# A four-layer graph network on one core: the first two quads of graphs in another order

## The chip, the cores and the metric

One core of a Trainium2 chip runs the whole program. Its engines work side by side, each through its own queue in program order: TensorE (PE; its weight loads are shown apart as PEld), VectorE (DVE), ScalarE (ACT), GpSimd (POOL) and SyncE (SP, which here only starts transfers). They wait for each other through semaphores. The metric is the device time of one execution in microseconds (us), the median of several runs; less is better. All data is 32-bit floating point.

## What is computed

128 graphs share one adjacency matrix of 128 nodes; each node has 256 features. Four layers follow each other, each with a residual and a normalization over the features:

```python
x = _layernorm(x + attention(x))     # layer 0: 512 edges, 4 heads; softmax over a node's edges; @ W_out.T
x = _layernorm(x + slconv(x))        # layer 1: three products with (adj*adj) @ . @ W1, W2, W3, relu between
x = _layernorm(x + split(x))         # layer 2: diagonal, upper, lower part of adj, each with its own W, + bias
x = _layernorm(x + gcn(x))           # layer 3: A_hat @ x, two products, batch norms over all graphs
```

In layer 0 an edge's score is `sum(a * leaky_relu(q[src] + q[dst])) + log(adj[src, dst] + 1e-8)`, the softmax runs over the edges that leave a node, and the weighted values are summed per node. Layer 3 normalizes over all graphs, so its end can only follow when all graphs are through its first part.

## The kernel before

The 128 graphs are taken in 32 groups of four, called quads. A pipeline works on several quads at once: `iteration(k)` does layer 1 of quad k, layers 2 and 3 of quad k - 1, the output of layer 0 of quad k + 1, the softmax of quad k + 2 and the query products of quad k + 3. Before that steady part stand `start()`, which loads everything, sorts the edges and takes the first quads through layer 0, and `iteration_0()`, which fills the pipeline. After it comes a last part for the batch norms and the output. The order of every engine's queue is the order in which the program writes the instructions (`manual_schedule`); no scheduler changes it. Tiles come from pools with a fixed number of buffers; a tile whose turn comes again waits until its last reader is done. [...]

The steps that the change and the prediction speak of, with the lines of the kernel before:

- `values_in(k)` (L235 on) transposes a quad on TensorE (L245) and copies it out (L247); `values(k, i)` makes queries and values of one graph (L259, copies at L260 and L261). After the last graph the queries are written to DRAM (L268), by SP or by POOL.
- `gather_one` (L336) fetches the queries of an edge's source rows, and then adds those of its target rows, by indirect transfers from POOL: chunk c of 128 edges needs a transfer for the sources (t = 0) and an adding one for the targets (t = 1). `gather` does chunks 0 to 2, `gather_last` chunk 3, which takes over a buffer of an earlier chunk.
- `score(k, c)` (L368, L370, L371) turns a gathered chunk into scores on VectorE: three passes over 128 x 1024 elements. L373 adds the edge weights of quads 0 and 1, L375 those of the later quads, after the last chunk.
- `sorted_scores` (L360) brings the scores of quads 0 and 1 into the sorted order with a permutation matrix that lies in the room of w3; so w3 can be loaded only when quad 1 is sorted. Later quads are gathered in sorted order already, and one transpose (L385, with copies at L387) does instead.
- `softmax_parts` (L389 to L400): two scans on VectorE for the maximum, a subtraction, an exponential on ScalarE (L396, which needs another table of functions), two scans for the sum. `attention` transposes the result (`pat`, L408) and divides (L410, L412).
- `scatter` (L418) writes the weights into a matrix in DRAM with four indirect transfers from POOL, each of which waits for the one before; `load_weights` (L427) reads it back through SP; `by_row` (L437) makes rows of it (ScalarE, or VectorE for quad 0); `aggregate` (`py`, L451) multiplies it with the values.
- `stage_a` (`po`, L465) is layer 0's output product, the residual (L468) and the norm (L106 to L121) for two graphs, then for the other two.
- `mix1` (`pm`, L476), `first` (`ph`, L490) and `mix2`/`mixed` (L532, L540 to L544) are layer 1's first product for quad 0; `first_seven` does the same for later quads with seven products instead of eight. `late_sums` (L548, L549), `second` (L575, seven products of blocks again; `between[i]` holds work that is put between its steps) and `third` (`p3`, L655), `third_mix` (L668), `third_norm` follow.
- `weight_blocks` (L188 to L191), `hidden_sums` and `second_sums` (L181 to L184) make the sums of weight blocks that the seven-product form needs, on VectorE.
- In `start()`: the first ten products on `warm` (L1091), `late_loads` with its small vectors for biases and batch norms (L1143, L1149), the copy at L1253 with which POOL waits for quad 0's weights.

Of the kernel before, what the change touches and what calls it, by code (L numbers as in the profile page):

```python
# [11 lines left out]
AF = mybir.ActivationFunctionType  # L12
# [14 lines left out]
def gnn_stack(ctx: ExitStack, tc: tile.TileContext, x, adj, w_qv_t, a, w_out_t, src, dst,  # L27
# [14 lines left out]
    nc = tc.nc  # L42
# [3 lines left out]
    P = 128  # L46
# [18 lines left out]
    def ps(name):  # L65
        return psum.tile([P, 512], F32, tag="ps", name=name)
# [57 lines left out]
    def layer_norm(pool, r):  # L124
        mv = norm_stats(pool, r)
        norm_apply(pool, r, mv, norm_root(pool, mv))


    with ExitStack() as phase:
# [210 lines left out]
        def gather_last(k):  # L340
            quads[k].z[NE - 1] = z_buffer(k, NE - 1)
            for t in range(2):
                gather_one(k, t, NE - 1)
# [113 lines left out]
        def stage_a(k):  # L457

            s = quads[k]
            yts = s.yts  # L460
            for j in range(0, QB, 2):
                po = ps("po").rearrange("p (b d) -> p b d", d=D)
                for t in range(2):
                    for dc in range(DC):
                        nc.tensor.matmul(po[:, t, :], yts[j // 2][:, t, dc, :], wo[:, dc, :],  # L465
                                         start=(dc == 0), stop=(dc == DC - 1))
                xj = s.xr[:, j:j + 2, :]
                nc.vector.tensor_add(xj, xj, po)  # L468
                layer_norm(wk, xj)
# [553 lines left out]
        def iteration_0():  # L1023

            late_sums(0)
            between = {i: [] for i in range(14)}
            between[0] = [lambda: attention(1), lambda: scatter(1)]
            for c, i in ((0, 1), (1, 3), (2, 6)):
                between[i].append(lambda c=c: score(2, c))
            between[1].append(lambda: gather_last(2))  # L1030
            for j, i in enumerate((10, 11, 12, 13)):
                between[i].append(lambda j=j: by_row(1, j))
            second(0, between)
            score(2, NE - 1)
            gather(3)
            rest = third(0, 0)
            next(rest)
            first_seven.blocks = weight_blocks(w1_sb, w1_s)
            layer2.blocks = weight_blocks(l2w, l2w_s)
            next(rest)  # L1040
            aggregate(1)
            queries.blocks = weight_blocks(wqv, wqv_s)
            hidden_sums()
            for _ in rest:
                pass
            stage_a(1)
            third_mix(0, 0)
            rest = third(0, 2)
            next(rest)
            third_norm(0, 0)  # L1050
            mix1(1, 0)
            mix1(1, 2)
            next(rest)
            w = first_seven(1)
            steps = softmax_parts(2)
            for _ in range(4):
                next(steps)
            w.p1()
            next(steps)
            run(w.p5, w.p2)  # L1060
            for _ in steps:
                pass
            next(rest)
            attention(2)
            scatter(2)
            score(3, 0)
            gather_last(3)
            w.p6()
            next(rest, None)
            w.p7()  # L1070
            third_mix(0, 2)
            w.p4()
            w.p3()
            quads[0].layer2 = layer2(0, 1)
            next(quads[0].layer2)
            third_norm(0, 2)
            next(quads[0].layer2)

        def start():
# [9 lines left out]
            warm = ps("warm")[:, :N]  # L1089
            for _ in range(10):  # L1090
                nc.tensor.matmul(warm, ones, ones, start=True, stop=True)  # L1091
# [47 lines left out]
            def late_loads():  # L1139
                for c in range(DC):  # L1140
                    nc.sync.dma_start(l2w[:, c, :].rearrange("p (k f) -> p k f", k=3),
                                      l2_w[:, c * P:(c + 1) * P, :].rearrange("k p f -> p k f"))
                nc.sync.dma_start(bias, bass.AP(tensor=l2_bias.tensor, offset=l2_bias.offset, ap=[[0, P], [1, D]]))  # L1143
                nc.sync.dma_start(w3_sb, w3.rearrange("(c p) f -> p c f", p=P))
                nc.sync.dma_start(l3w1, l3_w1_t.rearrange("(c p) f -> p c f", p=P))
                quads[4].xg = load_x(4, "xg", 1, xpool)
                for t, vecs in ((bn1, (l3_b1, l3_g1, l3_be1)), (bn2, (l3_b2, l3_g2, l3_be2))):
                    for i, ap in enumerate(vecs):
                        nc.sync.dma_start(t[:, i, :], ap.rearrange("(c p) -> p c", p=P))  # L1149

# [21 lines left out]
            nc.vector.scalar_tensor_tensor(weight, picked, LOG_EPS, count, op0=ALU.add, op1=ALU.mult)  # L1172
            nc.scalar.activation(weight, weight, AF.Ln)
# [11 lines left out]
            values_in(1, quads[1].xr, nc.scalar.copy)  # L1185
# [22 lines left out]
            score(0, NE - 1, ends[:, 3, :])  # L1208
            sorted_scores(0, perm, (NE - 1,))
# [16 lines left out]
            values_in(2, quads[2].xr, nc.scalar.copy)  # L1226
# [4 lines left out]
            nc.vector.tensor_add(an, a_sb, ident)  # L1231
            attention(0)
            values(2, 0, nc.scalar.copy, qt=l3w1_s.rearrange("p t f -> p (t f)").rearrange("p (b d) -> p b d", d=D))
# [10 lines left out]
            values(2, 1, nc.scalar.copy)  # L1244
            pr = ps("col_ps")[:, :1]
            nc.tensor.matmul(pr, an, ones[:, 0:1], start=True, stop=True)
            nc.vector.tensor_add(sums[:, 2:3], sums[:, 0:1], pr)
            nc.vector.tensor_sub(sums[:, 3:4], sums[:, 2:3], sums[:, 1:2])
            nc.scalar.activation(sums[:, 4:5], sums[:, 3:4], AF.Sqrt)
            score(1, 0, ends[:, 3, :])  # L1250
            values(2, 2, nc.scalar.copy)
# [3 lines left out]
            for c in (2, 3):  # L1255
                for t in range(2):
                    gather_one(1, t, c, cols_i[:, t, :])
            dinv = sums[:, 5:6]
            nc.vector.reciprocal(dinv, sums[:, 4:5])
            nc.vector.tensor_scalar(diag, an, dinv, None, op0=ALU.mult)  # L1260
            values_in(3, quads[3].xg, nc.scalar.copy)
            values(3, 0, nc.scalar.copy)
# [3 lines left out]
            score(1, 1, ends[:, 3, :])  # L1266
            values(3, 1, nc.scalar.copy)
            second_sums()
            for j in range(QB):
                by_row(0, j, None if j == 2 else nc.vector.tensor_copy)  # L1270
            aggregate(0)
            stage_a(0)
            values(3, 2, nc.scalar.copy)
            values(3, 3, nc.scalar.copy)
            mix1(0, 0)
            mix1(0, 2)
            score(1, 2, ends[:, 3, :])
            sorted_scores(1, perm, range(NE - 1))
            first(0, 0)
            score(1, NE - 1, ends[:, 3, :])  # L1280
            gather(2)
            first(0, 1)
            mixed(0, 0, mix2(0, 0))
            sorted_scores(1, perm, (NE - 1,))
            late_loads()
            first(0, 2)
            mixed(0, 1, mix2(0, 1))
# [3 lines left out]
            first(0, 3)  # L1291
            next(steps)
            mixed(0, 2, mix2(0, 2))
# [323 lines left out]
```

## Time and profile before

| | us |
|---|---|
| median of 3 runs (lowest, highest) | 3142.03 (3140.09, 3143.48) |
| the profiled execution's own time | 3137.62 |
| its span in the trace | 3135.9 |
| mean granted clock of TensorE | 0.995 of full speed |

The last three numbers belong to one execution, and rows of the profile are compared with its own time. What each engine did in stretches of the beginning (busy us, clock granted to TensorE, mean share of time in which the transfer engines were busy):

| stretch, us | TensorE | VectorE | ScalarE | POOL | clock | transfers |
|---|---|---|---|---|---|---|
| 30 to 40 | 8.93 | 9.79 | 3.16 | 0.78 | 1.00 | 0.13 |
| 40 to 50 | 4.21 | 8.18 | 1.57 | 5.34 | 0.77 | 0.74 |
| 50 to 60 | 9.65 | 5.05 | 4.94 | 3.79 | 0.89 | 0.19 |
| 60 to 70 | 2.70 | 8.85 | 2.38 | 3.49 | 0.79 | 0.42 |
| 70 to 80 | 9.41 | 3.92 | 1.47 | 2.59 | 0.70 | 0.62 |
| 80 to 90 | 8.86 | 9.33 | 2.55 | 4.60 | 1.00 | 0.70 |
| 90 to 100 | 10.00 | 5.25 | 3.67 | 4.65 | 1.00 | 1.01 |
| 100 to 110 | 6.61 | 8.85 | 2.31 | 1.75 | 1.00 | 1.03 |
| 120 to 130 | 10.00 | 3.20 | 5.51 | 3.54 | 1.00 | 0.84 |
| 140 to 150 | 7.57 | 8.67 | 2.12 | 1.43 | 1.00 | 0.64 |
| 150 to 160 | 4.02 | 8.30 | 3.71 | 1.33 | 0.90 | 0.00 |
| 160 to 170 | 9.99 | 7.19 | 2.91 | 4.01 | 0.76 | 0.01 |
| 190 to 200 | 10.00 | 9.47 | 2.69 | 0.00 | 1.00 | 0.00 |

In the rows of a timeline the first number is the start from the beginning of the span, the second the length; then come the engine, the line of the kernel, the operation, what it writes and reads with the shapes, the number of records (one matrix product of these types has two), and in brackets the idle time ahead of it with what ended it. A row of waits has the total in us, the number of waits and the longest one.

### The profile page before, as it was taken

What the parts mean: (1) busy time and instruction counts of PE and PEld (TensorE: products, weight loads), DVE (VectorE), ACT (ScalarE), POOL (GpSimd) and SP (SyncE); (2) the same over time, 40 slices, a digit from 0 to 9 for tenths busy, and PEclk for the clock granted to TensorE, in tenths of its full rate; (3) what the DMA queues carried; (4) which work ended last, traced back from release to release, by engine and by line L of the source; (5) the groups of instructions that cost most, each with busy time, mean ns of one, the idle gap of its engine ahead of it and who ended that gap; (6) DMA issues with size and microseconds to landing.
All of it is one profiled execution on the core that took longest, in us unless ns stands there. A gap on an engine that the chain in (4) does not pass through costs nothing. (4 is left out here: it accounts for less than half of the span.)

```text
span 3135.9 us, 39741 instructions
## 1 busy us (share of the span) xinstructions
PE 3070.0 (98%) x14752; PEld 2399.9 (77%) x14752; DVE 2307.2 (74%) x4600; ACT 1375.0 (44%) x2548; POOL 649.8 (21%) x535
## 2 busy tenths in 40 slices
PE   7899999999999999999999999999999999999987
PEld 3678888888888888888888888888888887874444
DVE  7777777777777777777777777777777776458888
ACT  3344433444444444443444444444343444326668
POOL 2311222222111111222222111111222220001135
PEclk8999999999999999999999999999999999999999
DMA  5623333333333323333333333223333331005557
GB/s 175 166 71 86 102 108 95 108 108 106 104 81 108 95 80 93 104 102 101 108 108 105 84 101 107 91 79 95 108 102 101 108 108 41 21 28 203 176 191 276
DMA packets 117473, 340.04 MB, mean 108 GB/s; under 512 B 14881, under 2 KB 51617, under 8 KB 108961
## 3 DMA queue, kind: packets, MB, share of 16 engines
q0 software_dynamic: 44544, 147.88, 19.4%
q1 hardware_dynamic: 70976, 188.71, 16.9%
q8 instruction: 117, 1.92, 0.3%
q10 hardware_dynamic: 1760, 0.92, 0.1%
q14 instruction: 76, 0.61, 0.1%
HBM read 252.00 MB, written 85.46 MB: 108 GB/s over the span
## 5 line engine op out<-in xcount | busy, mean ns | idle before, releaser
L575 PE MATMUL ph<-m,w 128*128 128x256 f32 x2048 | 473.4, 379 | 0.0
L655 PE MATMUL p<-w,h 128*128 128x256 f32 x2048 | 464.2, 380 | 0.0
L575 PEld LDWEIGHTS ph<-m,w 128*128 128x128 f32 x2048 | 386.7, 190 | 77.9 <-issue 14.8
L655 PEld LDWEIGHTS p<-w,h 128*128 128x128 f32 x2048 | 389.9, 190 | 67.0 <-issue 8.1
L336 POOL DMA_INDIRECT zs<-qd,src_idx x120 | 116.1, 968 | 1344.3 <-DMA qd<-qt 1214.1
L575 PE MATMUL ph<-m,w_s 128*128 128x256 f32 x1536 | 357.5, 379 | 0.0
L575 PEld LDWEIGHTS ph<-m,w_s 128*128 128x128 f32 x1536 | 291.8, 190 | 52.9 <-issue 14.8
L336 POOL DMA_INDIRECT zs<-qd,dst_idx x120 | 188.4, 1570 | 350.5 <-DMA zs<-qd,src_idx 325.3
L581 ACT COPY u<-ph 128x512 f32<-128x512 f32 x128 | 74.8, 584 | 354.9 <-PE ph L575 354.9
L418 POOL DMA_INDIRECT attd<-at,att_idx x128 | 140.7, 1099 | 353.1 <-DMA attd<-at,att_idx 251.5
L591 ACT ACTIVATE h<-h 128x512 f32<-128x512 f32 x192 | 121.2, 631 | 135.6 <-DVE h L587 135.6
L113 ACT ACTIVATE ln_sd<-ln_mv,eps 128x2 f32<-128x2 f32 x192 | 56.0, 291 | 280.2 <-DVE ln_mv L108 276.4
L370 DVE TENSOR_TENSOR zs<-zs,a_bc 128x1024 f32<-128x1024 f32 x125 | 153.1, 1225 | 4.3
L371 DVE TENSOR_REDUCE scores<-zs 128x16 f32<-128x1024 f32 x125 | 152.5, 1220 | 4.3
L718 ACT COPY x2k<-y 128x384 f32<-128x384 f32 x192 | 91.8, 478 | 138.6 <-PE y L711 114.3
L368 DVE SCALAR_TENSOR_TENSOR zs<-zs 128x1024 f32<-128x1024 f32 x125 | 151.4, 1212 | 1.1 <-DMA zs<-qd,dst_idx 1.1
L106 DVE BATCH_NORM_STATS2 ln_st<-xr 128x6 f32<-128x256 f32 x384 | 144.5, 418 | 6.6
L121 DVE TENSOR_SCALAR xr<-xr,ln_mv,ln_rs 128x256 f32<-128x256 f32 x384 | 143.3, 415 | 7.0
L587 DVE TENSOR_TENSOR h<-ph,u 128x512 f32<-128x512 f32 x128 | 87.1, 680 | 73.2 <-PE ph L575 54.9
L437 ACT COPY adc<-ad 128x512 f32<-128x512 f32 x125 | 133.4, 1067 | 5.5 <-DMA ad<-attd 5.5
L679 POOL TENSOR_TENSOR xb<-xr,bias 128x512 f32<-128x512 f32 x64 | 99.3, 1551 | 150.9 <-DVE xr L121 141.6
L532 PE MATMUL pm<-wt_t,h 128*128 128x128 f32 x1024 | 126.7, 277 | 0.0
(346 smaller groups left out, 6064.1 us busy)
## 6 DMA issues: line engine op xcount, KB each, us to landing
ad<-attd SPq DMA_DIRECT2D x32, 1024.0 KB, 4.8
zd<-z SPq DMA_DIRECT2D x31, 1024.0 KB, 7.5
zl<-zd SPq DMA_DIRECT2D x62, 512.0 KB, 3.8
xr<-in_x_dram SPq DMA_DIRECT2D x32, 512.0 KB, 7.3
x3d<-xr SPq DMA_DIRECT2D x32, 512.0 KB, 2.6
x3l<-x3d SPq DMA_DIRECT2D x32, 512.0 KB, 5.9
out_dram<-x3l POOLq DMA_DIRECT2D x31, 512.0 KB
qd<-qt SPq DMA_DIRECT2D x30, 512.0 KB, 2.6
```

Source lines behind the costliest of these rows:

```text
L106: nc.vector.bn_stats(st[:, i, :], r[:, i, :])
L121: nc.vector.tensor_scalar(r[:, i, :], r[:, i, :], mv[:, i, 0:1], rs[:, i:i + 1], op0=ALU.subtract, op1=ALU.mult)
L336: nc.gpsimd.indirect_dma_start(out=s.z[c], out_offset=None, in_=s.qd, in_offset=bass.IndirectOffsetOnAxis(ap=idx[:, c:c + 1], axis=0), com ...
L368: nc.vector.scalar_tensor_tensor(z, z, SLOPE, z, op0=ALU.mult, op1=ALU.max)
L370: nc.vector.tensor_mul(z3, z3, a_bc.unsqueeze(1).to_broadcast([P, QB, D]))
L371: nc.vector.reduce_sum(s.es[:, c, :], z.rearrange("p (r d) -> p r d", d=DH), axis=AX.X)
L418: nc.gpsimd.indirect_dma_start(out=ad, out_offset=bass.IndirectOffsetOnAxis(ap=att_idx[:, c:c + 1], axis=0), in_=s.at[:, c, :], in_offset= ...
L437: (copy or nc.scalar.copy)(s.adc[:, j * H:(j + 1) * H, :], s.ad.rearrange("p (s r) -> p r s", r=R)[:, j * H:(j + 1) * H, :])
L532: nc.tensor.matmul(pm[:, c // 2, c % 2, :], quads[k].h1[i, c], wt_t, start=True, stop=True)
L575: nc.tensor.matmul(bank[g][:, i].rearrange("p b n -> p (b n)"), wa[:, c, f:f + P], s.m2[:, blk_b, c].rearrange("p b n -> p (b n)"), start= ...
L591: nc.scalar.activation(h, h if src_ is None else src_, AF.Relu)
L655: nc.tensor.matmul(p3[:, t * D:(t + 1) * D], s.h2[f // 2][:, f % 2, j + t, :], w3_sb[:, f, :], start=(f == 0), stop=(f == K2 - 1))
```

## The change

Only `start()`, `iteration_0()` and `stage_a` are touched; the steady part and the end stay as they are. Nothing is computed otherwise. It does these things:

- `stage_a` falls into `out_product` (L462) and `out_norm` (L471), which for quad 0 are called apart: both products stand ahead of the first norm.
- In `start()`, quad 1's transposes go ahead of the logarithm, quad 2's transposes ahead of the last sorting product of quad 0, three of quad 2's four products ahead of quad 0's attention, and all of quad 3's products ahead of quad 0's weights; quad 3's queries are written to DRAM by POOL instead of SP.
- Two chunks of quad 1 are gathered in the order source, source, target, target instead of source, target, source, target.
- The scores of quad 1 go ahead of two small sums on VectorE that wait for a product of TensorE.
- Twenty products without use, of the kind of the first ten, stand ahead of quad 0's `aggregate`, and four ahead of its `mix1`.
- Quad 0's first layer-1 products are put in another order, and quad 1's four sorting products stand together behind them.
- The late loads follow behind these sorting products, w3 first; the small vectors go behind `second(0)` (`small_loads`). The weight sums of w1, l2w and l3w1 are put into `iteration_0` in other places, those of wqv into `start()`.
- In `iteration_0`, quad 1's attention and scatter stand behind three steps of `second(0)` instead of one; the scores of quad 2 are spread otherwise; `third(0, 0)` is issued in one piece; quad 2's softmax begins ahead of quad 1's output of layer 0.

```diff
-            between[0] = [lambda: attention(1), lambda: scatter(1)]
-            for c, i in ((0, 1), (1, 3), (2, 6)):
+            for c, i in ((0, 0), (1, 3), (2, 6)):
                 between[i].append(lambda c=c: score(2, c))
-            between[1].append(lambda: gather_last(2))
-            for j, i in enumerate((10, 11, 12, 13)):
-                between[i].append(lambda j=j: by_row(1, j))
+            between[2] += [lambda: attention(1), lambda: scatter(1)]
+            between[3].append(lambda: gather_last(2))
             second(0, between)
+            small_loads()
+            first_seven.blocks = weight_blocks(w1_sb, w1_s)
+            layer2.blocks = weight_blocks(l2w, l2w_s)
+            rest = third(0, 0)
+            next(rest)
             score(2, NE - 1)
             gather(3)
-            rest = third(0, 0)
-            next(rest)
-            first_seven.blocks = weight_blocks(w1_sb, w1_s)
-            layer2.blocks = weight_blocks(l2w, l2w_s)
-            next(rest)
-            aggregate(1)
-            queries.blocks = weight_blocks(wqv, wqv_s)
-            hidden_sums()
+            for j in range(QB):
+                by_row(1, j)
             for _ in rest:
                 pass
+            hidden_sums()
+            aggregate(1)
+            steps = softmax_parts(2)
+            for _ in range(4):
+                next(steps)
             stage_a(1)
             third_mix(0, 0)
             rest = third(0, 2)
             next(rest)
             third_norm(0, 0)
+            next(steps)
             mix1(1, 0)
+            next(rest)
             mix1(1, 2)
+            w = first_seven(1)
             next(rest)
-            w = first_seven(1)
-            steps = softmax_parts(2)
-            for _ in range(4):
-                next(steps)
             w.p1()
-            next(steps)
-            run(w.p5, w.p2)
             for _ in steps:
                 pass
-            next(rest)
+            run(w.p5, w.p2)
+            next(rest, None)
             attention(2)
             scatter(2)
+            w.p6()
             score(3, 0)
             gather_last(3)
-            w.p6()
-            next(rest, None)
...
+            score(1, 1, ends[:, 3, :])
...
             second_sums()
+            keep_running(20)
             for j in range(QB):
                 by_row(0, j, None if j == 2 else nc.vector.tensor_copy)
+            queries.blocks = weight_blocks(wqv, wqv_s)
             aggregate(0)
-            stage_a(0)
-            values(3, 2, nc.scalar.copy)
-            values(3, 3, nc.scalar.copy)
+            po = [out_product(0, j) for j in (0, 2)]
+            out_norm(0, 0, po[0])
+            keep_running(4)
             mix1(0, 0)
+            out_norm(0, 2, po[1])
+            first(0, 0)
+            score(1, 2, ends[:, 3, :])
+            first(0, 1)
             mix1(0, 2)
-            score(1, 2, ends[:, 3, :])
-            sorted_scores(1, perm, range(NE - 1))
-            first(0, 0)
+            mixed(0, 0, mix2(0, 0))
+            first(0, 2)
             score(1, NE - 1, ends[:, 3, :])
             gather(2)
-            first(0, 1)
-            mixed(0, 0, mix2(0, 0))
-            sorted_scores(1, perm, (NE - 1,))
+            first(0, 3)
+            mixed(0, 1, mix2(0, 1))
+            sorted_scores(1, perm)
             late_loads()
-            first(0, 2)
-            mixed(0, 1, mix2(0, 1))
+            pm = mix2(0, 2)
             steps = softmax_parts(1)
             for _ in range(4):
                 next(steps)
-            first(0, 3)
+            mixed(0, 2, pm)
             next(steps)
-            mixed(0, 2, mix2(0, 2))
             mixed(0, 3, mix2(0, 3))
             for _ in steps:
                 pass
```

`keep_running(n)` issues n products of `ones` with `ones` into a bank that nothing reads.

## Prediction

> **What bounds the kernel now.** I read the page first, then TensorE's own waits over the first 175 us, then the timeline of each engine there, then the stage windows.
>
> ```profile
> span 3135.9 us, 39741 instructions
> PE 3070.0 (98%) x14752; PEld 2399.9 (77%) x14752; DVE 2307.2 (74%) x4600; ACT 1375.0 (44%) x2548; POOL 649.8 (21%) x535
> ```
>
> TensorE is busy for 98% of the span, and after 174 us its timeline has no wait until the tail. Up to 174 us it has these (us in total, times, longest):
>
> ```profile
> PE pat L408 <- DVE pair L400: 14.8, 3, 6.0
> PE py L451 <- DVE adc L437: 7.9, 1, 7.9
> PE pe L360 <- DVE scores L373: 2.6, 2, 1.5
> PE pm L476 <- DVE xr L121: 2.4, 2, 1.8
> ```
>
> In TensorE's timeline (start, length, what, idle before it):
>
> ```profile
> 47.96 0.63 PE L408 MATMUL pat<-ident,pair 48*128 48x48 f32 x4 [5.37 <-DVE pair L400]
> 48.52 5.48 PE L259 MATMUL pq<-wqv,xt 128*128 128x512 f32 x8
> ...
> 70.59 3.68 PE L451 MATMUL py<-adc,m 128*64 128x128 f32 x32 [7.89 <-DVE adc L437]
> 74.20 4.61 PE L465 MATMUL po<-wo,yt 128*128 128x256 f32 x16
> ...
> 104.99 0.41 PE L408 MATMUL pat<-ident,pair 48*128 48x48 f32 x4 [3.39 <-DVE pair L400]
> ...
> 160.01 0.63 PE L408 MATMUL pat<-ident,pair 48*128 48x48 f32 x4 [5.99 <-DVE pair L400]
> ...
> 173.47 0.67 PE L697 MATMUL pt<-ident,xr 128*128 128x128 f32 x4 [1.22 <-DVE xr L121]
> ```
>
> The same products are slower after a long wait: eight pq take 5.48 here and 3.68 at 53.98; py takes 3.68 here and 1.97 at 131.43. The granted clock (third number from the end of a stage row; then the share of busy transfers, and GB/s) says why:
>
> ```profile
> 44.00:46.00 2.00, 0.00 (x0) 0.00 (x0) 1.58 (x6) 1.31 (x3) 1.46 (x2) 0.83 0.32 127
> 64.00:66.00 2.00, 0.00 (x0) 0.00 (x0) 1.97 (x3) 0.00 (x0) 0.00 (x0) 0.95 0.75 315
> 102.00:104.00 2.00, 0.00 (x0) 0.00 (x0) 1.97 (x4) 0.28 (x1) 0.00 (x0) 1.00 1.03 234
> ```
>
> So all there is to win is some 30 us of waits and half clock before 174 us. From there the work is the same and TensorE-bound, so the time moves one for one with the start of the last transposes that wait, now at 173.47. I walk the new order of each in-order queue to that instruction, with the durations and start-to-start distances of these rows.
>
> **1. Up to the first softmax (48 us): nothing.** Copying quad 1's transposes ahead of the logarithm frees TensorE 1.4 us earlier (24.99 to 23.57), but VectorE runs without a gap from 22.3 to 41.5 and the product at 40.42 waits for it. Quad 2's transposes (1.04) and three of its products (5.3) go into the 5.37 us ahead of pat. That wait shrinks to about 1 us, pat stays at 47.96, and the half clock of 45.3 to 52.1 goes. VectorE still makes quad 0's attention by 49.4.
>
> **2. Quad 0's weights (66.1 us): unmoved.** The four scatters (49.73, 54.11, 56.53, 59.14), the load at 61.26 and its arrival at 66.13, which ScalarE's copy shows, hang on that attention and on nothing moved. What moves is VectorE: score(1,0) waited at 54.42 for col_ps, a tiny product queued behind two pq. Now it needs only its gather, and the transfers are busy until 52 with both gathers, so the first has landed near 50.5. Scores 0 and 1 end at 58.6 (not 65.2), the four sums of w2 (4.67) at 64.3 (not 69.9), before the weights arrive. VectorE's first copy (0.62) lets py start at 66.75, not 70.59: 3.84 won.
>
> **3. Clock and quad 0's norms.** Twenty warming products (40 records; pm's show 0.12 each when fast) run from 59.3 to about 63.9 and leave 2.9 us idle. Cost if the cover were gone: at half clock they take 8 us (the first ten took 4.00) and hold py to 67.3. At full clock: py paced by VectorE's copies to 68.7, two po of 1.8 each to 72.3 (now 78.8). Both po stand ahead of the norm, whose first half takes 2.65: 70.6 to 73.25; four more warming products (0.9) lie inside that. The wqv sums (1.8 on VectorE) lie under po. Then pm 73.3, mx copied 75.0, two ph 78.6, pm, pm2, two ph, pm2 to 85.0, four pe (3.7) to 88.7. VectorE beside it: the gathers of quad 1 now go src, src, dst, dst, so the chunk-2 one lands near 78.9 (by busy transfers of 1.6 and 3 us from 72 on), score 2 runs to 83.0, a copy, score 3 to 87.7. That is just in time for the fourth pe. The pe of quad 1 ended at 93.5 before: 4.8 won.
>
> **4. Quad 1's softmax.** From the first scan to pat it took 8.0 us (96.95 to 104.99); now 88.75 to 96.3. Before, one product of second() stood ahead of pat; now three do (5.2 us, from 90.6 to 95.8), so the wait is 0.5 instead of 3.39. In TensorE work that is 8.7 + 3.4 = about 12 us won here.
>
> **5. What is late next.** The attention is now behind late sums, score(2,0), one sum: 96.2 + 1.4 + 3.75 + 0.6 + 0.7 = 102.7, only 4.3 earlier than 107.0. In second(), S4 must wait for VectorE's sum behind score(2,2): 0.9 lost, second ends at 116.8 (was 128.0), the whole third(0,0) at 123.9. Scatter, load and last gather of quad 1 and 2 keep their distances from the attention:
>
> ```profile
> 107.30 1.75 POOL L418 DMA_INDIRECT attd<-at,att_idx  x1 [10.59 <-DVE at L412]
> ...
> 123.68 1.59 POOL L336 DMA_INDIRECT zs<-qd,dst_idx  x1 [3.66 <-DMA zs<-qd,src_idx]
> ```
>
> Score(2,3) started at 129.88 waiting for that gather; 4.3 less is 125.6, done at 129.6. The new order puts the transpose of quad 2's scores (L385, before at 149.34) ahead of po, third_mix and mix1. TensorE, done with py at 126.7 (load 121.9, four copies of 1.07), waits 2.9 us there, and all of stage_a(1) behind it waits too. The w1 and l2w sums (4.1) fill VectorE while the gather flies: no cost.
>
> **6. To the end of iteration 0.** Hidden sums and two scans plus a subtraction follow (to 134.3), then three norms of 2.9 to 143.0 (now 149.7). ScalarE then has a table load (1.28) and exp (0.63) ahead of both mx copies: first product y at 144.6, a wait of 1.9. The last scans end at 149.1, pat starts at 149.2 (was 160.01) with third's second half done ahead of it. The half clock there (two groups of 2.07 and 3.05 against 1.03 and 1.89) goes. Score(3,0) (3.75) again holds VectorE, so the last hidden sum comes at 156.5; from that sum to the waiting transposes it took 169.27 to 173.47, so they start at 160.7. Gain 12.8. Each hand-over costs 0.03 to 0.1 in these rows and I rounded some away: I take **12 us**.
>
> **Loads.** All late loads now stand behind the sorting of quad 1 on SP (88.8 instead of 83.25 on), with w3 first; third needs it at 116.8. Transfers were full from 84 to 110 (27 us of busy share, of which I estimate 9.4 the loads). The gathers of quad 2 start earlier, so I estimate them done by 102, loads by 105. SP's load of quad 1's weights queues behind them, free at 115.7; the small bias and vector loads queue behind that, the bias being needed at 143. Quad 3's spill moves from SP's queue (82.87) to POOL's, between the gathers of quads 1 and 2, for 0.6 of issue (as the one at 66.73); quad 2's first gather still finds its buffer before 84. Cost zero; if the cover is gone, see rivals.
>
> **A rule against a row.** [...] idle from 42.58, the clock fell within 2.7 us (0.83 in 44 to 46), while a gap of 3.39 at 101.6 kept 1.00. [...] by the row, where it falls, py and po pay about 2.3 more. I take the clock as held, being a bit likelier, and keep both.
>
> **Rivals.**
> - *Clock falls before py* (0.27): gain 9.7, 3132.3. For it, the fall at 45.3; against it, the gap at 101.6.
> - *Given back at L385* (0.14): the loads keep the transfers full past 103, each of quad 1's scatters takes the 4.21 of its first hop (107.30 to 111.51) instead of 3.16, 2.39 and 2.94: 4.1 later, score(2,3) with it: gain near 8, or 4 if the last gather loses as much again; 3134 to 3138, at 3136 in the middle. Against: after 110 the transfers' share was 0.10.
> - *It does not do what it says* (0.04): iteration 1 hangs on VectorE and the lead is eaten. VectorE is 74% busy, so against. Gain near 0, 3142.
> - *Slower* (0.03): score(2,0) stands ahead of the attention on VectorE. If its gather shares the transfers with the block of loads and lands only with the last of them, at 110 + 6 (they start 6 later) = 116 instead of before 97.6, 18.4 us are lost against 12 won: about 3148. It turns at a landing of 109.6. Against it: the gather is issued some 3 us before the first load.
>
> **Numbers.** The profiled execution took 3137.6 (span 3135.9); the median of the runs is 3142.0, so I subtract from the median. Likeliest (0.52): 3142.0 - 12 = **3130.0**, by itself 3127 to 3133. The range takes in a fallen clock, most of L385, and shorter scatter hops (up to 3 us more gain): 3125.5 to 3137.5. About 0.2% (6.3 us, 3135.7) can be told from no change: faster 0.52 + 0.27 + 0.07 = 0.86, same 0.07 + 0.04 = 0.11, slower 0.03.
>
> **What would show it.** py near 66.8 and at half the length; clock 1.00 from 40 to 174; pat of quad 1 near 96.3 with a wait under 1; a wait of about 3 at L385 for VectorE's scores near 129.6; about 2 ahead of y for ScalarE; pt near 160.7. Wrong if the scores of quad 1 or 2 start on a wait for a transfer, if L385 ends after 135, or if TensorE waits after 161.

## The result and the profile after

The kernel after takes **3130.56 us** (median of four runs, 3128.09 to 3134.48) against 3142.76 for the kernel before in the same comparison (four runs, 3140.09 to 3146.52): a ratio of 0.9961, 95% interval 0.9944 to 0.9979. That is 12.2 us, where 12 had been forecast. The profiled execution of after took 3130.48, with a span of 3128.8.

The head of its page answers to that of before:

```profile
span 3128.8 us, 39836 instructions
PE 3075.6 (98%) x14800; PEld 2401.8 (77%) x14800; DVE 2316.9 (74%) x4600; ACT 1375.8 (44%) x2548; POOL 652.3 (21%) x536
```

TensorE's own waits over the first 175 us of after (what waited, for what, total, times, longest):

```profile
PE pe L385 <- DVE scores L375: 3.8, 1, 3.8
PE pe L360 <- DVE scores L373: 1.8, 1, 1.8
PE y L289 <- ACT mx L484: 1.7, 1, 1.7
PE pat L408 <- DVE pair L400: 1.3, 2, 1.1
PE py L451 <- DVE adc L437: 1.3, 1, 1.3
PE pt L702 <- DVE xr L121: 1.2, 1, 1.2
```

pat waits 1.3 in all instead of 14.8 and py 1.3 instead of 7.9. New at the top are L385 and y, the two that the prediction named. TensorE's timeline of after at the places shown of before:

```profile
47.56 0.41 PE L408 MATMUL pat<-ident,pair 48*128 48x48 f32 x4 [1.09 <-DVE pair L400]
...
48.62 3.66 PE L259 MATMUL pq<-wqv,xt 128*128 128x512 f32 x4
...
66.53 1.97 PE L451 MATMUL py<-adc,m 128*64 128x128 f32 x32 [1.32 <-DVE adc L437]
...
96.10 0.41 PE L408 MATMUL pat<-ident,pair 48*128 48x48 f32 x4 [0.26 <-DVE pair L400]
...
130.27 0.30 PE L385 MATMUL pe<-ident,scores 128*128 128x128 f32 x1 [3.77 <-DVE scores L375]
130.40 5.31 PE L467 MATMUL po<-wo,yt 128*128 128x256 f32 x16
...
161.13 0.67 PE L702 MATMUL pt<-ident,xr 128*128 128x128 f32 x4 [1.22 <-DVE xr L121]
```

The last transposes that wait, called **the mark** from here on, start at 161.13 instead of 173.47: 12.34 us earlier. po behind L385 is 5.31 long, against 3.72 for the same sixteen products at 68.43. The stage rows say why (granted clock third from the end):

```profile
50.00:52.00 2.00, 2.00 (x3) 0.57 (x2) 1.97 (x3) 0.00 (x0) 0.28 (x1) 0.50 0.75 145
130.00:132.00 2.00, 1.73 (x6) 1.41 (x7) 1.85 (x6) 1.34 (x5) 1.56 (x2) 0.64 0.02 2
132.00:134.00 2.00, 2.00 (x6) 1.64 (x5) 1.97 (x2) 0.97 (x1) 1.70 (x2) 0.51 0.87 262
```

Two half-clock stretches are left: one behind pat of quad 0, which was to vanish, and one behind the new wait at L385, which had not been foreseen.

Two questions follow. What sets the mark, if it moved by the forecast amount although TensorE lost some 1.6 us at L385 that was not in the sum? And why do the two profiled executions differ by only 7.1 us of span (3135.9 - 3128.8), when the mark differs by 12.3 and the medians by 12.2?

**Theory.** The mark is set by VectorE's chain: it begins when the last gather of quad 2 lands (score(2,3)) and goes through the scans, three norms, mx, sums, scans, score(3,0) and the last norm. **Rival one:** the mark is TensorE's own sum of waits, as the prediction's count of "TensorE work won" has it. **Rival two:** one part (the start, the order of iteration 0, the loads, the warming) makes the gain alone.

VectorE's timelines of before and of after show where that chain begins and what stands behind it:

```profile
129.88 1.23 DVE L368 SCALAR_TENSOR_TENSOR zs<-zs 128x1024 f32<-128x1024 f32 x1 [1.10 <-DMA zs<-qd,dst_idx]
...
133.80 0.42 DVE L188 TENSOR_TENSOR w_s<-w 128x256 f32<-128x256 f32 x1
...
140.94 0.68 DVE L468 TENSOR_TENSOR xr<-xr,po 128x512 f32<-128x512 f32 x1
```

```profile
126.12 1.23 DVE L368 SCALAR_TENSOR_TENSOR zs<-zs 128x1024 f32<-128x1024 f32 x1 [5.08 <-DMA zs<-qd,dst_idx]
...
130.04 0.42 DVE L181 TENSOR_TENSOR l3w_s<-l3w 128x256 f32<-128x256 f32 x1
...
131.70 1.21 DVE L389 TENSOR_TENSOR_SCAN m<-reset_f,pair 16x512 f32<-16x512 bf16 x1
```

In before, 7.1 us of weight sums (w1, l2w, wqv, l3w) follow score(2,3); in after only 1.7 us of them (l3w), as the others have moved into the wait for the gather or into the start. That is 5.5 of the 8.6 us by which the chain from score(2,3) to the mark is shorter.

### The profile page after: what moved, and what is told of

Read it like the earlier page. It is cut to its first block, busy times and chain, and to the rows that moved or that the text cites. A ratio compares the mean times of both kernels' runs of the same rounds, so it can differ in the third digit from the quotient of the medians.

```text
span 3128.8 us, 39836 instructions
## 1 busy us (share of the span) xinstructions
PE 3075.6 (98%) x14800; PEld 2401.8 (77%) x14800; DVE 2316.9 (74%) x4600; ACT 1375.8 (44%) x2548; POOL 652.3 (21%) x536
## 5 line engine op out<-in xcount | busy, mean ns | idle before, releaser
L580 PEld LDWEIGHTS ph<-m,w 128*128 128x128 f32 x2048 | 386.8, 190 | 77.9 <-issue 14.8
L580 PEld LDWEIGHTS ph<-m,w_s 128*128 128x128 f32 x1536 | 291.7, 190 | 53.6 <-issue 14.8
L106 DVE BATCH_NORM_STATS2 ln_st<-xr 128x6 f32<-128x256 f32 x384 | 144.6, 419 | 6.6
```

The source lines that it names most:

```text
L106: nc.vector.bn_stats(st[:, i, :], r[:, i, :])
L580: nc.tensor.matmul(bank[g][:, i].rearrange("p b n -> p (b n)"), wa[:, c, f:f + P], s.m2[:, blk_b, c].rearrange("p b n -> p (b n)"), start= ...
```

## The experiments

One row for each kernel. The ratio is to the kernel before in the same comparison, on the same chip; its own median there was 3142.76 for the row of after and 3139.6 to 3140.4 for the others. The medians of different rows are from several chips, so the ratios are to be compared. The last four columns are from the one profiled execution of each kernel. "Gather" is the start of score(2,3), "chain" the time from there to the mark. In e5 and e11 score(2,3) starts without a wait, behind VectorE's own work, and not on the landing. A long sum is explained with the ninth experiment.

| kernel | median us | ratio, 95% interval | gather | mark | chain | long sums |
|---|---|---|---|---|---|---|
| before | 3142.76 | 1 | 129.88 | 173.47 | 43.59 | 0 |
| after | 3130.56 | 0.9961 (0.9944 to 0.9979) | 126.12 | 161.13 | 35.01 | 5 |
| e1_order_alone | 3136.00 | 0.9983 (0.9977 to 0.9990) | 133.13 | 171.34 | 38.21 | 2 |
| e2_start_alone | 3136.09 | 0.9986 (0.9980 to 0.9993) | 124.97 | 167.04 | 42.07 | 3 |
| e3_no_warming | 3133.74 | 0.9974 (0.9963 to 0.9984) | 128.55 | 163.70 | 35.15 | 6 |
| e4_loads_early | 3129.17 | 0.9969 (0.9958 to 0.9981) | 126.40 | 161.40 | 35.00 | 2 |
| e5_one_product | 3129.58 | 0.9970 (0.9957 to 0.9982) | 125.60 | 160.90 | 35.30 | 2 |
| e6_products_first | 3127.68 | 0.9966 (0.9952 to 0.9980) | 124.67 | 159.66 | 34.99 | 1 |
| e7_exp_first | 3127.46 | 0.9956 (0.9942 to 0.9970) | 124.87 | 158.22 | 33.35 | 5 |
| e8_all_three | 3128.64 | 0.9961 (0.9947 to 0.9975) | 125.41 | 159.38 | 33.97 | 3 |
| e9_sum_between | 3127.00 | 0.9954 (0.9936 to 0.9971) | 127.12 | 162.12 | 35.00 | 0 |
| e10_both | 3125.73 | 0.9950 (0.9937 to 0.9964) | 127.07 | 160.42 | 33.35 | 0 |
| e11_before_between | 3140.17 | 1.0001 (0.9992 to 1.0009) | 130.19 | 174.50 | 44.31 | 1 |
| e12_before_again | 3141.41 | 1.0005 (0.9997 to 1.0013) | 130.20 | 174.13 | 43.93 | 0 |

The intervals of most versions of after overlap; between them the marks and chains decide. In these traces the copies of quad 0's weights let py start anywhere from 65.62 to 67.02 in kernels whose work up to there differs by nothing, by warming products or by loads alone, so a mark by itself is good to about 1 us, and a chain, which starts at its own landing, to about 0.3 (34.99 to 35.01 in four kernels; 43.59 and 43.93 in two executions of the kernel before).

### The two halves apart

e2 is after with iteration 0 as before, except that the small loads stay behind second(0); e1 is the reverse, before with iteration 0 in its new order, the small loads staying in the start and the wqv sums behind the hidden sums.

```diff
 e2, in iteration_0
-            between[2] += [lambda: attention(1), lambda: scatter(1)]
+            between[0] = [lambda: attention(1), lambda: scatter(1)]
...
-            steps = softmax_parts(2)
-            for _ in range(4):
-                next(steps)
             stage_a(1)
...
             w = first_seven(1)
+            steps = softmax_parts(2)
+            for _ in range(4):
+                next(steps)
```

> Iteration 0 in its new order, the start as before. Mark: the last transposes of iteration 0 that wait (pt<-ident,xr), at 173.47 us before and 161.13 after; their difference of 12.3 is the lead. Theory (the start's order wins some 8.7 us of it and iteration 0's order some 3.5, each by itself): pat of quad 1 stays near 105 with a wait under 1 instead of 3.39, its attention on VectorE then stands behind score(2,0), the last gather of quad 2 comes some 4 us later and L385 near 138; from L385 to the mark it took 30.9 after, so the mark lies near 169, time near 3138. Rival (the order of iteration 0 is the change, and the start's lead would be lost without it): the mark at 166 or earlier.

> The start in its new order, iteration 0 as before (the small loads behind second(), quad 1's wqv sums in the start). Theory: pe of quad 1 ends at 88.7 as after, pat of quad 1 at 96.3 but with its old wait of 3.4 to 4, as one product stands ahead of it; from there to the mark 68.5 us as before: the mark near 164.8, time near 3133.5. Rival (the lead is lost on the way, VectorE being the bound of iteration 0 in its old order): the mark at 170 or later.

Both marks came 2.2 to 2.3 us later than the theory said (171.34 for 169, 167.04 for 164.8). In e1, VectorE has the wqv sums (1.7) ahead of the scans, and z and x of the first seven, behind a wait of 1.85, took 1.79 and 1.91 instead of 1.10 and 1.03 in after. In e2 the attention comes at 98.4, and its scatters begin while the late loads and the gathers of quad 2 keep the transfers full (a share of 1.01 to 1.08 from 98 to 104). GpSimd's timeline of e2:

```profile
98.91 1.75 POOL L418 DMA_INDIRECT attd<-at,att_idx  x1 [7.18 <-DVE at L412]
105.56 1.01 POOL L418 DMA_INDIRECT attd<-at,att_idx  x1 [4.90 <-DMA attd<-at,att_idx]
```

That hop is 6.65, against 4.21 in before and 4.09 in after (102.65 to 106.74). What follows: neither half makes the gain alone (2.1 and 6.4 of 12.3), and 3.8 come only from both. The table shows how: the start brings the gather earlier (129.88 to 124.97) and leaves the chain long (42.07); the order makes the chain short (38.21) and the gather late (133.13). Rival two falls as far as these two parts go. The medians split the gain otherwise: e1 and e2 are 4.3 and 4.2 us under the 3140.3 of before on that chip, where 3138 had been expected of e1 and 3133.5 of e2. The split by the mark comes from one execution of each kernel.

### Warming and loads

e3 is after without both calls of keep_running; e4 issues the loads of l2w and l3w ahead of keep_running(20), where SP reaches them at 61.85.

```diff
 e3
-            keep_running(20)
-            keep_running(4)
 e4
+            early_loads()
             keep_running(20)
```

> After without the twenty and the four warming products. Theory (the clock falls in the gap before py, py and po run at half clock on the chain to quad 0's norms): granted clock about 0.5 from 62 to 70, py 3.7 instead of 1.97 long or paced by its copies, po 5.5 or more instead of 3.72; the fourth pe and the mark 2.0 to 3.5 us later, the mark at 163.1 to 164.6. Rival (the norms on VectorE and the last chunk of scores hide it): the mark within 0.5 of 161.1.

> After with the loads of l2w and l3w (1.3 MB) issued at about 60 us, ahead of the load of quad 0's attention copies, instead of behind the sorting of quad 1. Theory (their place matters because they share the transfers with quad 1's chunk-2 and chunk-3 gathers): these land 3 to 6 us later, score(1,2) starts at 82 to 85 instead of 79, the mark at 164 to 167. Rival (the place of the loads is worth nothing by itself, as these gathers have slack or the loads end before them): the mark within 0.7 of 161.1.

e3 went as its theory had it: 163.70, or 2.6 later. Its TensorE timeline, and then a stage row:

```profile
67.02 3.68 PE L451 MATMUL py<-adc,m 128*64 128x128 f32 x32 [5.82 <-DVE adc L437]
```

```profile
66.00:68.00 2.00, 0.98 (x10) 1.01 (x12) 1.97 (x5) 1.06 (x1) 1.29 (x3) 0.56 0.00 0
```

py takes 3.68 instead of 1.97 and po 4.90 instead of 3.72; the fourth pe ends at 91.97 instead of 88.68. The gather lands 2.4 later, and the chain is as long as ever. Of the 2.6, 0.5 is a later arrival of quad 0's weights in that execution (py could start at 67.02 instead of 66.53), so the warming products are worth 2.1 to 2.6 us.

e4 went to its rival: the mark at 161.40, within 0.3. Its theory was right in kind: score(1,2) starts at 79.94 instead of 78.61, and pat of quad 1 comes 0.9 later (97.01). But it is given back: the first hop of quad 1's scatters takes 3.17 (103.56 to 106.73) instead of 4.09. Fewer loads are left beside that hop, which may be why; no row shows it. So the loads of l2w and l3w gain nothing by standing behind the sorting rather than at 62 us. Their place in before (83 to 104) was not tried by itself, and neither was the new place of the small loads.

### Which wait is on the path

Three single edits in iteration 0 of after, and all together with the hidden sums ahead of score(2,3):

```diff
 e5
-            between[2] += [lambda: attention(1), lambda: scatter(1)]
+            between[0] = [lambda: attention(1), lambda: scatter(1)] + between[0]
 e6
+            po = [out_product(1, j) for j in (0, 2)]
             steps = softmax_parts(2)
...
-            stage_a(1)
+            for i in range(2):
+                out_norm(1, 2 * i, po[i])
 e7
-            for _ in range(4):
+            for _ in range(5):
                 next(steps)
             stage_a(1)
...
-            next(steps)
             mix1(1, 0)
 e8, besides those of e6 and e7
             next(rest)
+            hidden_sums()
             score(2, NE - 1)
...
-            hidden_sums()
             aggregate(1)
```

> After with quad 1's attention and scatters behind one product of second() and ahead of score(2,0), as before, instead of behind three and behind score(2,0). Theory A (what the two more products win at pat is given back at L385): pat waits 3.5 to 4 instead of 0.26, but the attention, the scatters and quad 2's last gather come 4 to 5 us earlier, L385 starts near 130 with no wait and po keeps the full clock; the mark (161.13 after) at 160 to 162. Theory B (as predicted, the three products win 3.4 us for good): the mark near 164.5.

> After with quad 1's two output products ahead of the transpose of quad 2's scores (L385) instead of behind it. Theory A (the wait at L385 of 3.8 and the half clock behind it are not on the path; VectorE's chain from quad 2's last gather is): po runs from 126.6 to 130.2 at full clock, L385 at 130.3, pm of quad 1 still at 138 with a new wait of 4 to 5; the mark at 160.5 to 161.5. Theory B (TensorE's wait and half clock are the path): the mark 1.7 to 5.5 earlier.

> After with the exponential of quad 2 ahead of quad 1's norms on ScalarE, right behind the subtraction. Theory A (between 138 and 161 ScalarE's table load of 1.28 and exponential of 0.63 ahead of the mx copies are on the path): y starts 1.5 to 2 us earlier than 145.21, the table load at 158.75 ahead of the last root goes too; the mark at 157.9 to 159.5. Theory B (the norms are later by the table load that now lies ahead of their first root, VectorE being the bound): the mark at 160.8 to 162.

> After with three edits: output products ahead of L385, the exponential ahead of the norms, and the hidden sums ahead of score(2,3), where VectorE waits 5.1 us for the last gather. Theory A (VectorE's chain from that gather on sets the mark): hidden sums of 1.6 leave the chain only in part, as ScalarE's four copies of pe (1.07) then show; with the edit on the exponential the mark at 156 to 158, time 3 to 5 us under the kernel after. Theory B (another chain, the scatters and the load, sets it): the mark at 160 or later.

**e5** settles the place of the attention: behind one product, pat of quad 1 waits 3.71 and the mark is at 160.90, not later. What after wins at pat it gives back at L385, which in e5 starts at 129.74 with no wait. Two things meet in e5. Its attention is 4.1 us earlier, though the earlier scatters lose on their first hop (98.56 to 105.39). But second() and the weight sums behind it are later, and so score(2,3) does not wait for its gather at all. VectorE's timeline of e5:

```profile
125.12 0.56 DVE L191 TENSOR_TENSOR l2w_s<-l2w,l2w_s 128x384 f32<-128x384 f32 x1
125.60 1.22 DVE L368 SCALAR_TENSOR_TENSOR zs<-zs 128x1024 f32<-128x1024 f32 x1
```

The gather had landed at 124.64. In this order VectorE's own queue, fed by TensorE's second(), is nearly as late as the landing, and an earlier gather alone would win nothing more.

**e6** settles L385. Without the wait ahead of it po ends at 128.4 (135.71 in after), and yet the chain is 34.99. VectorE's and TensorE's timelines of e6:

```profile
124.67 1.22 DVE L368 SCALAR_TENSOR_TENSOR zs<-zs 128x1024 f32<-128x1024 f32 x1 [4.04 <-DMA zs<-qd,dst_idx]
```

```profile
136.14 1.52 PE L481 MATMUL pm<-wt_t,xr 128*128 128x128 f32 x8 [4.45 <-DVE xr L121]
...
159.66 0.67 PE L702 MATMUL pt<-ident,xr 128*128 128x128 f32 x4 [1.22 <-DVE xr L121]
```

The wait has moved to pm (4.45, for VectorE's norm), and the products behind it are slow (third's eight take 3.22, against 1.89 in after). Its mark of 159.66 lies between the two theories; it is 1.47 earlier than after's because the gather landed 1.45 earlier in that execution. Rival one falls: of TensorE's losses at L385, 3.8 of wait and 1.6 of clock, nothing reaches the mark.

**e7** went with its theory A, the mark at 158.22: it shortens the chain itself by 1.65 us, to 33.35. The rest of the 2.9 at the mark is a gather that landed 1.25 earlier in that execution. ScalarE's timeline, and then TensorE's:

```profile
133.86 0.63 ACT L396 ACTIVATE pair<-pair 16x512 f32<-16x512 f32 x1 [3.30 <-DVE pair L394]
134.51 1.28 ACT L113 ACT_TABLE_LOAD   x1
```

```profile
158.22 0.64 PE L702 MATMUL pt<-ident,xr 128*128 128x128 f32 x4
```

One table load of 1.28 now stands ahead of the first norm's root and costs VectorE 0.76 instead of 0.36 there; two others are gone (142.62 and 158.75 in after). The mark's transposes no longer wait at all.

**e8** did not add up: 159.38, outside the 156 to 158 expected. The chain is 33.97, 0.6 longer than with e7's edit alone, because products-first brings its wait to pm (4.84, then 2.05 for the eight products, against 1.05 in after), which delays the second mx copy. The hidden sums taken off the chain show as a wait for ScalarE's copies of pe (1.58) instead.

### Where the rest of the lead went

In after's profiled execution TensorE has a wait that before's does not have at all, in five iterations: y of layer 2 for ScalarE's copy x2k, 0.6 to 0.7 each:

```profile
PE y L716 <- ACT x2k L723: 3.3, 5, 0.7
```

VectorE's timeline of after in the first of them:

```profile
334.82 0.28 DVE L181 TENSOR_TENSOR x2s<-x2t 128x128 f32<-128x128 f32 x1
335.14 2.66 DVE L182 TENSOR_TENSOR x2s<-x2s,x2t 128x128 f32<-128x128 f32 x1
```

and GpSimd's:

```profile
334.75 1.59 POOL L336 DMA_INDIRECT zs<-qd,dst_idx  x1 [5.37 <-DMA zs<-qd,src_idx]
335.77 1.87 POOL L684 TENSOR_TENSOR xb<-xr,bias 128x512 f32<-128x512 f32 x1
```

A sum of 128x128 takes 2.66 us instead of 0.29, from just behind the start of GpSimd's second issue to just behind the end of GpSimd's own sum. The iteration then takes 86.64 to 86.73 instead of 85.74. e9 puts the sum xb between the two issues; e10 adds e7's edit; e11 is before with e9's edit; e12 is before again, for a second profiled execution.

```diff
 in iteration
-                gather_last(g)
+                gather_last(g, (0,))
...
             third_norm(c, 2)
+            if has_g:
+                gather_last(g, (1,))
```

The second argument names the ends to gather, 0 for the source and 1 for the destination; xb is the last step of third_norm.

> After with one change in every iteration from 1 on: GpSimd's sum xb (xr plus bias, rows 2 and 3) stands between the two issues of the last gather instead of behind both. In the profiled execution of after, five of 29 iterations have one VectorE sum of layer 2 (x2s, 128x128) that takes 2.65 us instead of 0.29; each begins 0.3 to 0.4 us after GpSimd's second issue (1.59) begins, with xb (1.88) right behind it, and ends when xb ends; TensorE then waits 0.66 and the lead falls by 0.9 to 1.0. Theory A (GpSimd and VectorE hold each other up there, and xb behind the issue makes it long enough to be felt): no x2s sum over 1.9 us, the mark at 161.1 as after, and from there to the end 2962.5 to 2963.5 as in the execution of before that has no such sum (after: 2967.7), time 3125 to 3127. Theory B (the sum xb, now 2 us earlier, meets other sums of VectorE in each iteration instead): a loss of 0.3 to 1.3 in each, time 3135 to 3160. Theory C (GpSimd has nothing to do with it): three to six long sums as before, time 3129 to 3132.

> After with the exponential of quad 2 ahead of quad 1's norms (as in e7_exp_first) and the sum xb between the two issues of the last gather in every iteration from 1 on (as in e9_sum_between). If the two are independent: first product of layer 2 (y<-l2w) near 159.6 as in e7, no long x2s sum, then 2961 to 2963.5 to the end as in e9 and in the profiled execution of before; time 3122.5 to 3125, all runs within 2 us of each other. If e7's gain of 2.9 at the mark is lost in iteration 1: 3126.5 to 3127.5, as e9.

> The kernel before with that one edit alone (xb between the two issues of the last gather). If the scatter of before's own runs (3138.04 to 3146.74) is the number of long x2s sums in each, about 0.93 us apiece: all runs within 2 us of each other, at 3137 to 3139, about 3 under before's median; and then the change by itself is worth about 11 to 12 us, e11 against e9. If the long sums are a matter of after's order alone: the median and the scatter of before stay as they are, 3140 to 3143.

> The kernel before, unchanged, for a second profiled execution. Open after e11: the one edit took the long x2s sums out of before's iterations and left its median and scatter as they were. Theory A (before has some two to five long sums in a usual execution, the first profiled one had none by chance): two or more long sums here, each iteration with one 0.85 to 1 us longer than 85.74. Theory B (they are rare in before, and its scatter is made in the first 175 us and in the tail after the last layer-2 product, where the executions so far differ by 1.2 and 2.7 us): none or one long sum, first product of layer 2 between 174.9 and 176.5, the tail 340.0 to 342.8.

**e9** followed theory A: no long sum, all its iterations without one, from mark to end 2963.5, and four runs within 0.75 us (3126.53 to 3127.28) where after's four span 6.4. GpSimd's xb now meets another sum, in every iteration, and there it costs nothing. VectorE's and GpSimd's timelines of e9:

```profile
333.99 1.28 DVE L182 TENSOR_TENSOR adc<-adc,x2t 128x128 f32<-128x128 f32 x1
```

```profile
333.84 1.28 POOL L685 TENSOR_TENSOR xb<-xr,bias 128x512 f32<-128x512 f32 x1 [2.30 <-DVE xr L121]
338.09 1.60 POOL L336 DMA_INDIRECT zs<-qd,dst_idx  x1 [2.97 <-DMA zs<-qd,src_idx]
```

That sum is 1.0 longer than usual, and TensorE never waits for it; 2.4 longer was felt.

Is it the issue that holds VectorE up, or xb behind it? The new order tells. All long sums lie in iterations whose second issue begins between 0.43 us before and 0.34 us after the first of the four x2s sums. In 36 of the 84 iterations of e9, e10 and e11 that have the new order it begins in that span too, and none of the four sums takes more than 0.34. One of these iterations, from GpSimd's and VectorE's timelines of e9:

```profile
1534.39 1.28 POOL L685 TENSOR_TENSOR xb<-xr,bias 128x512 f32<-128x512 f32 x1 [3.56 <-DVE xr L121]
1537.36 1.73 POOL L336 DMA_INDIRECT zs<-qd,dst_idx  x1 [1.69 <-DMA zs<-qd,src_idx]
```

```profile
1537.65 0.29 DVE L182 TENSOR_TENSOR x2s<-x2s,x2t 128x128 f32<-128x128 f32 x1
```

So the issue alone does not make the sum long; it takes xb right behind it.

**e10** has e7's short chain, no long sum, and the lowest median, 3125.73. It missed its expectation of 3122.5 to 3125, and its runs are 3.4 wide instead of 2 (3123.81 to 3127.17). In its profiled execution the gather lands 2.2 later than in e7, of which the first hop of its scatters makes 1.9 (5.49 instead of 3.56). The time from the start of layer 2's last round of products to the end (the tail) is 342.7. Among all fourteen profiled executions the tail goes with TensorE's clock: 340.1 to 340.2 in the six in which the granted clock falls to half once before the last 6 us, 340.5 to 342.7 in the eight in which it falls twice. The three at 342.7 are e7, e8 and e10, the kernels with e7's edit; whether the edit has a part in that stays open. e10 beats the kernel before (0.9950). That it beats after is likely by its trace but not shown by times, as the two intervals overlap.

**e11** was a miss: the same edit leaves before where it was (3140.17, runs from 3137.47 to 3143.43; its one long sum is in iteration 0, which keeps the old order), and **e12** shows why: before has few long sums to lose. Its second profiled execution has none either, and still its runs span 3137.80 to 3146.85. So long sums do not explain before's scatter as far as profiled executions show it; what does stays open.

## Why the prediction was right

**The start (parts 1 to 3): right.** py at 66.53 (66.75 forecast), po to 72.1 (72.3), pm 73.28 (73.3), fourth pe to 88.68 (88.7), each with the full clock (1.00 from 60 to 90). The half clock that was to vanish around 48 did not: it came back at 48.6 to 52, and the warming products ran from 60.58 to 65.2 instead of 59.3 to 63.9. This was hidden, as nothing on the path uses TensorE there. Instead of 2.9 us the gap ahead of py was 1.3. A reading of before was off without harm: VectorE is busy from 22.3 to 40.4, not to 41.5, and then waits 1.12 for the product at 40.42.

**The clock before py: held, but by luck.** That it would hold was an estimate, from two rows of before that pull apart. The gap of 2.9 us that was weighed never came; the warming products ran 1.3 later, because of the half clock that was not expected, and so left only 1.3. What 2.9 us would have done was not tried. The price of a fall, put at 2.3, measured 2.1 to 2.6 at the mark in e3.

**Quad 1's softmax (part 4): times right, worth wrong.** pat at 96.10 with a wait of 0.26 (96.3 and 0.5 forecast). The stretch from the first scan to pat was 8.0 in before and was put at 7.55 without a reason; it took 7.38. But "about 12 us won here", with 3.4 of it for two more products ahead of pat, was not a sum of independent terms: e5 shows that their place, paid for with a later attention, is worth nothing at the mark.

**What is late next (part 5): the times right within half a microsecond, by two errors that cancel.** The attention ended at 102.36 (102.7 forecast), score(2,3) started at 126.12 (125.6), the wait at L385 was 3.77 (2.9). The distances in between were not kept. From the first scatter to the gather's first issue it took 11.03 instead of 11.73, so the given-back rival did not occur there; but from the gather's second issue to its landing it took 8.01 instead of 6.20. The first hop was long where it was issued earlier (6.65 in e2, at 98.91 into transfers with a share of 1.01 to 1.08; 6.83 in e5, at 98.56), and after's later attention escaped the worst of it (4.09, at 102.65).

**To the end (part 6): right, with one omission.** y at 145.21 with a wait of 1.68 (144.6 and 1.9), pat at 149.87 (149.2), mark at 161.13 (160.7). The omitted term is the half clock behind L385, 1.6 us of TensorE. It did no harm, because the walk followed VectorE and not TensorE from there on (e6). What the walk's result rests on is the late landing of the gather by 0.5.

**Loads: zero cost held for l2w and l3w (e4), but probably not for the small loads.** They now stand on SP beside the last gather of quad 2. SP's and GpSimd's timelines of after:

```profile
115.10 0.42 SPq L1092 DMA_DIRECT2D bias<-in_l_bias_dram  x1
...
119.62 2.53 SPq L1095 DMA_DIRECT2D bn<-in_l_be_dram  x1
```

```profile
118.11 1.69 POOL L336 DMA_INDIRECT zs<-qd,dst_idx  x1 [3.44 <-DMA zs<-qd,src_idx]
```

In the ten kernels with the small loads there (after, e2 to e10) that gather takes 8.0 to 8.4 us from its second issue to its landing; in the four that issue them before 110 (before, e1, e11, e12) it takes 6.2 to 7.1. No run moved the small loads alone, so the cause is not shown; the place of a gather's landing at the head of the chain makes it worth trying.

**The signs.** "Clock 1.00 from 40 to 174" failed twice (0.50 in 50 to 52, and 0.51 in 132 to 134, behind L385). One sign of being wrong was badly put: score(1,2) and score(2,3) do start on a wait for a transfer (1.99 and 5.08), but the walk itself had them so.

**After the mark: not seen.** "TensorE waits after 161" was to prove the step wrong, and it did wait, five times. The five iterations are 4.65 us longer together, so this execution shows 7.1 of the mark's 12.3 (most of the other 0.6 are differences of 0.1 to 0.2 in two more iterations and the tail). The profiled execution of before was also 5.1 under the median of its runs, for which no cause was found, and so the medians still differ by 12.2. That the number came within 0.2 of the forecast is therefore luck: a loss of 5.2 behind the mark, which the prediction had at nothing, met a median of before that lay 5.1 above its profiled execution. The interval of the ratio goes from 6.6 to 17.6 us. What the walk had right is the mark, 12.34 against 12.8.

## What to carry to other kernels

When engines are coupled through in-order queues, find the landing that starts the last chain, and measure each edit by two numbers: when that landing comes, and how long the chain behind it is. A wait on the busiest engine may be worth nothing, even with a half clock behind it (3.8 and 1.6 us at L385). And two halves of a reordering may each give far less than both (2.1 and 6.4 of 12.3 us here): one moves the landing, the other makes the chain short.

## What the runs showed of the hardware

- **GpSimd held up VectorE.** With the old order of GpSimd's queue there are 322 iterations in the profiled executions (29 in each of eleven, and iteration 0 of e9, e10 and e11), and 30 have a long sum (2.66 us instead of 0.29 in the one shown). They are just the 30 in which the second issue began in the span named above. With the new order it began there 36 times, and no x2s sum took more than 0.34: the issue alone did not hold VectorE up, only the issue with xb right behind it. A sum beside xb alone was held up less: in e9 one begins 0.15 behind xb and takes 1.28, as xb does, instead of 0.29. In what way the two engines hold each other up is not shown, and why the long sums begin 0.4 to 0.7 us ahead of xb's recorded start stays open.
- **The clock fell behind short waits too.** In after it fell at about 48.6 (1.00 in 46 to 48, 0.66 in 48 to 50), when TensorE had waited 1.09 and 0.43 with only pat's four 48x48 transposes (0.41) between them, and was back at 52 (0.99 in 52 to 54). In the 2 us from 46 to 48 TensorE was busy for 0.88. In e3 the clock stood at 1.00 from 62 to 66 with no product at all and fell only then (0.56 in 66 to 68). The length of one wait does not tell.
- **A scatter issued into full transfers was slow to hand over (6.65 us in e2).** From the first to the second scatter of quad 1 it took 6.83 and 6.65 us when the first was issued at 98.56 and 98.91 (e5, e2), 5.49 at 101.82 (e10), and 3.17 to 4.21 in the eleven other kernels, at 102.03 or later. In e2 the transfers' share stayed at 1.01 to 1.08 until 104, 5 us behind the issue; in after, issued at 102.65, it was 1.05 in 102 to 104 and 0.32 in the next 2 us.
